# An RWKV attention and Hadamard FFN kernel: another order of work at the start, and three sets of weight forms made one block later

## The chip, the cores and the metric

The kernel runs on one core of a Trainium2 chip. A time is that of the whole program on the device, in microseconds (us), and smaller is better. The core has five engines that run their own instruction streams: TensorE (PE, matrix products into the eight PSUM banks), VectorE (DVE), ScalarE (ACT), GpSimd (POOL) and SyncE (SP), which here issues every DMA. Each stream is worked off in its order, and an instruction that waits holds up all that stand behind it on the same engine.

## The reference, cut to what matters

The input is 4 sequences of 2048 tokens with 512 channels, in 32-bit floats. What is computed:

```python
xn = layernorm(x)                                   # over the 512 channels of a token, no weights
shifted = xn of the token before (zero at a sequence's first)
xr, xk, xv = (mu * xn + (1 - mu) * shifted for mu in (mu_r, mu_k, mu_v))
r, k, v = xr @ Wr.T, xk @ Wk.T, xv @ Wv.T           # 512 x 512 each
wkv = a recurrence over the tokens with running maximum, numerator and denominator
attn = (sigmoid(r) * wkv) @ Wo.T
hidden = silu(xn @ W1.T) * (xn @ W3.T)              # 2048 wide
ffn = fwht(hidden) @ W2.T                           # Walsh-Hadamard transform over the 2048
out = x + attn + ffn
```

## The kernel before, in words

The 8192 tokens are worked off in 8 blocks of TB = 1024 tokens; two blocks make a sequence. Channels lie on the partitions, tokens along the free dimension, so `xnT` holds a block as 4 channel groups of 128 by 1024 tokens.

Each large product is done on 2 x 2 quarters with seven products in place of eight (`seven`, `down`). That needs seven *forms* of each weight, four of them the weight's quarters and three or four made by adding and subtracting quarters (`seven_forms` and `forms_in`, four POOL instructions of 128x256 for one tile). A *part* is one tile of seven forms (896 KB): there are 6 for k, v and r (`part_w` rows 0 to 5) and 16 for the FFN's first layer (rows 6 to 21). Forms are made once and kept in DRAM (`part_w`, `down_w`); later blocks load them from there. A part is loaded into `ring_a`, a pool of three buffers, so the load of a part must wait until the part three before it has been read for the last time. `ring_b` is a pool of two larger buffers, through which pass the square weights of block 0, the down weights and the tiles in which forms are made.

A normal block (1 to 7) goes: six calls of `projected_pair` (k, k, v, v, r, r; 14 matmuls each), sixteen of `up` (14 matmuls each), then `down`, seven products of 20 matmuls. During `down`, pieces of the next block's preparation are called between the products (`next_tokens`: statistics, normalizing, mixing), and at the last product `next_parts` loads the next block's first two parts.

Block 0 differs. Its k, v and r are plain products of 4 matmuls per 128x512 output (`projected`, 8 outputs for each of k, v, r). Beside them W2 is folded with the Hadamard matrix: `fold_load` brings W2 in eight pieces of 512 KB into the upper half of `hid`, `fold_products` multiplies each piece by the 128x128 Hadamard matrix `had_sb` (two matmuls a piece, and two ACT instructions that bring the result back), and `fold_butterflies` does the rest of the transform on VectorE. In the `up` loop of block 0 `down_forms` makes the forms of the down weights in steps 0 to 9, and `keep_parts` the six forms of k, v and r in steps 10 to 15: SP loads the quarters into a `ring_b` buffer, POOL makes the forms, SP stores the tile into `part_w`.

The opening works in two halves of 512 tokens. For each, `statistics` takes mean and variance on VectorE with tokens on the partitions, a power on POOL, writes scale and shift for each token to DRAM (`stat_d`) and reads them back broadcast to all partitions (`spread`); `normalize` applies them with two instructions for each channel group (two groups on VectorE, two on POOL), and `mixed(1)` makes k's mixed input in `tf`: for each group one ACT instruction and one VectorE instruction. The second half is normalized when k's products of the first half have been issued (the branch `n == NB`).

The order on each engine is that of the program text: every engine is wrapped in `InOrder`, which keeps program order. PSUM banks are given out in turn, eight of them. The profile puts every instruction on line 34, the line of that wrapper, so groups are told apart by their tiles: `bank<-tf,w` is k in block 0, `bank<-hid,w` v and r, `bank<-hid,had_sb` the folding, `bank<-xnT,part` and `bank<-tf,part` the `up` products, `bank<-hid,dw` the down products.

Of the kernel before, what the change touches and what calls it, by code (L numbers as in the profile page):

```python
# [8 lines left out]
F32 = mybir.dt.float32  # L9
AF = mybir.ActivationFunctionType  # L10
ALU = mybir.AluOpType
# [3 lines left out]
P = 128  # L15
# [24 lines left out]
def tile_rwkv_attn_hadamard_ffn(  # L40
# [7 lines left out]
    w2: bass.AP,  # L48
    wo: bass.AP,
    had: bass.AP,  # L50
    outT: bass.AP,
    n_batch: int,
):
# [49 lines left out]
    vec = const.tile([P, 5, NB], F32, name="vec")  # L103
    omm = const.tile([P, 3, NB], F32, name="omm")
    weff = const.tile([P, NB], F32, name="weff")
    had_sb = const.tile([P, P], F32, name="had_sb")
    neg_half = const.tile([P, TP], F32, name="neg_half")
    carry = const.tile([P, NB, 3], F32, name="carry")


    def load_tokens(i, t0=0, n=TB):
        dst = x_tok[:, t0 // P : (t0 + n) // P, :]
        sp.dma_start(out=dst, in_=x[ds(i * TB + t0, n), :].rearrange("(p t) c -> p t c", p=P))

    def load_channels(i, t0=0, n=TB):
        dst = xnT[:, :, OFF + t0 : OFF + t0 + n]
        sp.dma_start(out=dst, in_=xT[:, ds(i * TB + t0, n)].rearrange("(b p) t -> p b t", p=P))

    def statistics(i, t0=0, n=TB):

        m, key = n // P, f"{i}_{t0}"
        st = small.tile([P, TP, nc.vector.BN_STATS_DIM], F32, tag="st", name=f"st_{key}")
        mv = small.tile([P, TP, nc.vector.BN_AGGR_DIM], F32, tag="mv", name=f"mv_{key}")
        rs = small.tile([P, 2, TP], F32, tag="rs", name=f"rs_{key}")
        for t in range(m):
            dve.bn_stats(out=st[:, t, :], in_=x_tok[:, t0 // P + t, :])
        for t in range(m):
            dve.bn_aggr(out=mv[:, t, :], in_=st[:, t, :])
        dve.tensor_scalar(rs[:, 0, 0:m], mv[:, 0:m, 1], EPS, None, ALU.add)
        pool.tensor_tensor(rs[:, 0, 0:m], rs[:, 0, 0:m], neg_half[:, 0:m], ALU.pow)  # L130
        dve.scalar_tensor_tensor(rs[:, 1, 0:m], mv[:, 0:m, 0], -1.0, rs[:, 0, 0:m], ALU.mult, ALU.mult)
        far = stat_d[i, :, t0 : t0 + n]
        sp.dma_start(out=far.rearrange("s (p t) -> p s t", p=P), in_=rs[:, :, 0:m])
        sp.dma_start(out=spread[:, :, t0 : t0 + n], in_=far.unsqueeze(0).to_broadcast([P, 2, n]))

    def token_before(i):
        if i % per_batch == 0:
# [1 line left out]
        else:  # L139
            dve.tensor_copy(xnT[:, :, OFF - 1 : OFF], xnT[:, :, OFF + TB - 1 : OFF + TB])  # L140

    def normalize(t0=0, n=TB):
        for b in range(NB):
            eng = dve if b < KH else pool
            for s, op in ((0, ALU.mult), (1, ALU.add)):
                xb = xnT[:, b, OFF + t0 : OFF + t0 + n]
                eng.tensor_tensor(xb, xb, spread[:, s, t0 : t0 + n], op)

    def mixed_block(kind, b, t0=0, n=TB):
        m = mix_of[kind][:, b, t0 : t0 + n]  # L150
# [1 line left out]
        act.activation(m, before, AF.Copy, scale=omm[:, kind, b : b + 1])  # L152
        dve.scalar_tensor_tensor(m, here, vec[:, kind, b : b + 1], m, ALU.mult, ALU.add)

    def mixed(kind, t0=0, n=TB):
        for b in range(NB):
            mixed_block(kind, b, t0, n)


    def load_square(i, kind):  # L160
# [142 lines left out]
    def forms_in(t):  # L303
        seven_forms([t[:, n] for n in range(3, 7)], *(t[:, n] for n in range(4)))

    def load_parts(i, n):
        t = ring_a.tile([P, 7, KH, P], F32, tag="a", name=f"part_{i}_{n}")
        if i:
            sp.dma_start(out=t, in_=part_w[n])
        else:  # L310
            sp.dma_start(out=t[:, 0:4], in_=wpart[n])
            forms_in(t)
        return t

    def keep_parts(n):
        t = ring_b.tile([P, 7, KH, P], F32, tag="b", name=f"keep_{n}")
        sp.dma_start(out=t[:, 0:4], in_=wpart[n])
        forms_in(t)
        sp.dma_start(out=part_w[n], in_=t)

    def projected_pair(i, n, w, tail, hook):

        kind, g = (1, 2, 0)[n // KH], n % KH
        dst = (r_sb, k_sb, v_sb)[kind]
        d11, d12, d21, d22 = (dst[:, mh * KH + g, ts(t, H)] for mh in range(2) for t in range(2))

        def out(d, p):
            if kind == 0:
                act.activation(d, p, AF.Tanh, scale=0.5)
            else:  # L330
                act.copy(d, p)

        def on11(pa):
            out(d11, pa)
            hook()

        def on22(pa, pb, s5):
            dve.tensor_tensor(d22, pb, s5, ALU.add)
            hook()

        def on12(pc, s5):
            dve.tensor_tensor(d12, pc, s5, ALU.add)
            hook()

        pb, pc, pd = seven(f"{i}_r{n}", w, right_of[kind], tail, on11, on22, on12)
        left = [lambda: out(d21, pd)]
        if kind == 0:
            left += [lambda: out(d22, d22), lambda: out(d12, d12)]
        return left

    def up(i, j, w, tail, step):


        if i == 0:
            sp.dma_start(out=part_w[3 * KH + j], in_=w)

        h0, h1 = hid[:, j, 0:H], hid[:, j, H:TB]

        def on11(pa):
            act.activation(h0, pa, AF.Tanh, scale=0.5)  # L360

        def on22(pa, pb, s5):
            dve.scalar_tensor_tensor(h0, h0, 1.0, pa, ALU.add, ALU.mult)
            step()
            dve.tensor_tensor(pb, pb, s5, ALU.add)

        def on12(pc, s5):
            dve.tensor_tensor(pc, pc, s5, ALU.add)
            step()

        pb, pc, pd = seven(f"{i}_{j}", w, right_of["up"], tail, on11, on22, on12)
        return (
            lambda: act.activation(h1, pc, AF.Tanh, scale=0.5),
            lambda: dve.tensor_tensor(h0, h0, pd, ALU.mult),
            lambda: dve.scalar_tensor_tensor(h1, h1, 1.0, pc, ALU.add, ALU.mult),
            lambda: dve.tensor_tensor(h1, h1, pb, ALU.mult),
        )
# [142 lines left out]
        product(6, pb, y21, False, c21)  # L520


    load_tokens(0, 0, H)
    sp.dma_start(out=had_sb, in_=had)
    load_channels(0, 0, H)
    sp.dma_start(out=vec, in_=vecs.rearrange("p (v c) -> p v c", v=5))
    w_next = load_square(0, 1)
    pool.memset(neg_half, -0.5)
    statistics(0, 0, H)
    fold_load(0, 2)  # L530
    load_tokens(0, H, H)
    load_channels(0, H, H)
    fold_load(2, 4)
    fold_products(0, 2)
    dve.tensor_scalar(omm, vec[:, 0:3, :], -1.0, 1.0, ALU.mult, ALU.add)
    act.activation(weff, vec[:, 3, :], AF.Exp)
    token_before(0)
    normalize(0, H)
    mixed(1, 0, H)
    statistics(0, H, H)  # L540
    dve.tensor_scalar(weff, weff, -1.0, None, ALU.mult)

    pending = {}
    for i in range(n_blocks):
# [13 lines left out]
        if i == 0:  # L558
            for kind, after in ((1, 2), (2, 0), (0, None)):
                w = w_next  # L560
                if after is not None:
                    w_next = load_square(i, after)
                    if kind != 1:
                        mixed(after)
                if kind == 2:
                    token_forms()
                    fold_load(4, NP)
                for n in range(2 * NB):
                    if kind == 1:
                        if n == NB:  # L570
                            fold_products(2, 4)
                            normalize(H, H)
                            mixed(1, H, H)
                            mixed(2)
                        projected(kind, w, n % NB, n // NB)
                    else:
                        projected(kind, w, n // 2, n % 2)
                    if kind == 2 and n == 2:
                        fold_products(4, NP)
                        folded = fold_butterflies()  # L580
            parts = [load_parts(i, 3 * KH + n) for n in range(2)]
        else:

            def r_chores():
                for b in range(NB):
                    mixed_block(0, b)
                    yield
                yield from mix_forms(0)

            for kind in (1, 2):  # L590
                next(pending[kind])
            chores, hooks = r_chores(), [0]
            for n in range(3 * KH):
                parts.append(load_parts(i, n + 2))
                if n == KH:
                    token_forms()

                def hook():
                    hooks[0] += 1
                    if n <= KH:  # L600
                        next(chores, None)
                    if hooks[0] in (9, 11, 12, 14, 15, 17, 18):
                        step()

                tail = projected_pair(i, n, parts.pop(0), tail, hook)
# [3 lines left out]
        for j in range(NF):  # L609
            if i == 0 and j < NR:  # L610
                down_forms(j, folded)
            if i == 0 and j >= NF - 3 * KH:
                keep_parts(j - NF + 3 * KH)
            if j + 2 < NF:
                parts.append(load_parts(i, 3 * KH + j + 2))
            if j >= NF - 2:
                w_down.append(load_down(i, order[j - NF + 2]))
            tail = up(i, j, parts.pop(0), tail, step)
# [85 lines left out]
```

## Time and profile before

| | us |
|---|---|
| Median of three runs (3148.56 to 3155.57) | 3153.32 |
| The profiled execution | 3154.58 |
| Its span (first to last instruction) | 3152.4 |
| PE busy in it, 7224 matmul records | 3111.9 (99%) |
| DVE busy | 2200.6 (70%) |
| ACT busy | 871.6 (28%) |
| POOL busy | 338.5 (11%) |
| PE's first matmul starts at | 19.14 |
| First `up` product of block 0 starts at | 125.91 |
| First down product of block 0 starts at | 329.36 |

One 128x512 matmul in 32-bit floats shows as two matmul records; in the steady parts records follow one another every 0.43 us, so a matmul takes 0.86 us of PE. "Idle before" is the time for which an engine had nothing to do before an instruction, with what ended it.

### The profile page before, as it was taken

How to read it: one execution, taken by the hardware profiler on the slowest of the kernel's cores; microseconds unless marked ns; L12 is line 12 of the kernel's file. 1: busy time of each engine (PE TensorE's matmuls, PEld its weight loads, DVE VectorE, ACT ScalarE, POOL GpSimd, SP SyncE). 2: the span in 40 equal slices, each digit the busy share in tenths (PEclk: the TensorE clock that was granted, in tenths of full speed). 3: DMA queues.
4: the chain of work that ended last, by engine and by line, in shares of the span. 5: the costliest groups of instructions: out<-in, count | busy, mean ns of one | idle time of the engine just before them, and what ended most of it. 6: DMA issues, size and time to landing. Idle time of an engine off the chain costs nothing.

```text
span 3152.4 us, 20196 instructions
## 1 busy us (share of the span) xinstructions
PE 3111.9 (99%) x7224; PEld 1375.3 (44%) x7224; DVE 2200.6 (70%) x2300; ACT 871.6 (28%) x1366; POOL 338.5 (11%) x210
## 2 busy tenths in 40 slices
PE   6999999999999999999999999999999999999999
PEld 2443444444444444444444444444444444444444
DVE  5798756886478864787647876579655886658852
ACT  3233113331233302333023320333213332133310
POOL 3355301001000011000110001100011000110000
PEclk9999999999999999999999999999999999999999
DMA  4255632233322332223332224222332223322222
GB/s 174 94 167 199 236 107 70 82 125 110 108 81 77 118 127 102 82 70 114 133 107 79 73 102 157 95 70 82 128 124 101 72 82 145 123 74 81 75 101 77
DMA packets 76691, 340.93 MB, mean 108 GB/s; under 512 B 9776, under 2 KB 18864, under 8 KB 66992
## 3 DMA queue, kind: packets, MB, share of 16 engines
q1 hardware_dynamic: 76592, 339.65, 30.7%
q8 instruction: 57, 0.93, 0.1%
q14 instruction: 42, 0.34, 0.0%
HBM read 293.41 MB, written 46.20 MB: 108 GB/s over the span
## 4 chain that ended last, share of the span: by engine, by line
PE 96%; DMA 2%; POOL 1%; DVE 1%; SPq 0%; issue 0%; ACT 0%; POOLq 0%; DVEq 0%
PE bank L34 96%; POOL keep L34 1%; DMA keep<-wpart 0%; POOL part L34 0%; DMA xnT<-xT 0%; DMA part_w<-keep 0%; DMA dw<-down_w 0%; DVE xnT L34 0%; DMA part<-wpart 0%; DMA stat_d<-rs 0%; DMA k_sb<-x 0%; DVE st L34 0%; DMA v_sb<-stat_d 0%; DVE tf L34 0%; SPq L34 0%
## 5 line engine op out<-in xcount | busy, mean ns | idle before, releaser
L34 PE MATMUL bank<-tf,part 128*128 128x512 f32 x2272 | 1043.0, 592 | 0.0
L34 PE MATMUL bank<-hid,dw 128*128 128x512 f32 x1792 | 790.4, 594 | 4.6 <-DMA dw<-down_w 3.9
L34 PE MATMUL bank<-xnT,part 128*128 128x512 f32 x1536 | 723.9, 594 | 6.7 <-DMA part<-wpart 6.7
L34 PEld LDWEIGHTS bank<-tf,part 128*128 128x128 f32 x2272 | 432.0, 190 | 544.6 <-issue 514.3
L34 ACT COPY bank<-bank 128x512 f32<-128x512 f32 x526 | 299.8, 570 | 1261.5 <-PE bank L34 1255.6
L34 PEld LDWEIGHTS bank<-hid,dw 128*128 128x128 f32 x1792 | 341.4, 191 | 435.7 <-issue 432.0
L34 PEld LDWEIGHTS bank<-xnT,part 128*128 128x128 f32 x1536 | 292.0, 190 | 375.9 <-issue 365.7
L34 DVE SCALAR_TENSOR_TENSOR hid<-hid,bank 128x512 f32<-128x512 f32 x256 | 173.9, 679 | 181.6 <-ACT hid L34 181.5
L34 DVE TENSOR_TENSOR hid<-hid 128x1024 f32<-128x1024 f32 (+1 forms) x173 | 222.3, 1311 | 108.0 <-PE bank L34 107.0
L34 PE MATMUL bank<-hid,part 128*128 128x512 f32 x616 | 271.2, 592 | 0.0
L34 DVE RECIPROCAL e1b<-e1b 128x512 f32<-128x512 f32 x64 | 214.1, 3347 | 1.1
L34 PE MATMUL bank<-r_sb,dw 128*128 128x512 f32 x448 | 210.5, 592 | 0.0
L34 DVE TENSOR_TENSOR bank<-bank,s 128x512 f32<-128x512 f32 x256 | 168.0, 690 | 36.5 <-ACT bank L34 25.3
L34 ACT ACTIVATE hid<-bank 128x512 f32<-128x512 f32 x272 | 163.2, 600 | 98.3 <-PE bank L34 79.7
L34 POOL TENSOR_TENSOR rs<-rs,neg_half 128x8 f32<-128x8 f32 (+1 forms) x9 | 13.6, 1510 | 1577.0 <-DVE rs L34 1577.0
L34 DVE TENSOR_TENSOR hid<-hid,bank 128x512 f32<-128x512 f32 x256 | 173.5, 678 | 11.5 <-PE bank L34 7.1
L34 PEld LDWEIGHTS bank<-hid,part 128*128 128x128 f32 x616 | 117.0, 190 | 147.3 <-issue 145.4
L34 DVE SCALAR_TENSOR_TENSOR hid<-xnT,vec,hid 128x1024 f32<-128x1024 f32 x64 | 93.8, 1500 | 100.4 <-ACT hid L34 100.4
L34 PEld LDWEIGHTS bank<-r_sb,dw 128*128 128x128 f32 x448 | 85.1, 190 | 107.1 <-issue 106.7
L34 POOL TENSOR_TENSOR tf<-xnT 128x1024 f32<-128x1024 f32 x16 | 45.5, 2843 | 667.6 <-PE bank L34 667.6
L34 DVE TENSOR_TENSOR v_sb<-bank,v_sb 128x512 f32<-128x512 f32 x32 | 22.0, 688 | 135.9 <-PE bank L34 135.9
L34 ACT COPY s<-bank 128x512 f32<-128x512 f32 x128 | 75.1, 586 | 146.3 <-PE bank L34 146.3
(93 smaller groups left out, 2225.4 us busy)
## 6 DMA issues: line engine op xcount, KB each, us to landing
part<-part_w SPq DMA_DIRECT2D x154, 896.0 KB, 4.6
dw<-down_w SPq DMA_DIRECT2D x56, 1280.0 KB, 6.3
part_w<-part SPq DMA_DIRECT2D x16, 896.0 KB, 7.1
k_sb<-x SPq DMA_DIRECT2D x7, 2048.0 KB, 8.5
xnT<-xT SPq DMA_DIRECT2D x7, 2048.0 KB, 10.3
v_sb<-xT SPq DMA_DIRECT2D x48, 256.0 KB, 3.8
out<-v_sb SPq DMA_DIRECT2D x48, 256.0 KB, 2.0
part<-wpart SPq DMA_DIRECT2D x16, 512.0 KB, 5.4
```

Of the source, the lines that this page charges most:

```text
L34: return self.tc.keep_in_program_order(issue(*args, **kwargs))
```

## The change

Three things change in the program; the `up` parts of block 0 are handled as before.

1. In the opening, the first block's scale and shift no longer pass through DRAM. `first_spread` builds diagonal matrices from them (an identity `eye_sb` times the per-token value: four on VectorE, four on ACT, for each half) and multiplies them by a matrix of ones on TensorE, which leaves the values broadcast to all partitions in two PSUM banks. `first_normalized` then goes channel group by channel group: two VectorE instructions with the PSUM bank as an operand, and at once the mixing of that group. POOL no longer normalizes in the opening. The statistics of the first half are computed from two loads of 256 tokens.
2. W2's pieces are loaded earlier and folded in another order: pieces 0 and 1 are loaded ahead of the first channels, 2 and 3 just behind them, 4 to 7 after the second half's loads. Pieces 0 to 3 are multiplied before k's first product, 4 and 5 between k's halves, 6 and 7 in v.
3. `keep_parts` is no longer called in the `up` loop with a load and forms of its own. The k, v and r parts are made in block 1 instead: `load_parts` there brings the quarters (512 KB) and makes the forms in the ring buffer, and `projected_pair` stores the tile into `part_w`.

```diff
-    def statistics(i, t0=0, n=TB):
+    def token_statistics(key, tok):
...
+    def load_first_tokens(t, m):
+        src = x[ds(t * P, m * P), :].rearrange("(t p) c -> p t c", p=P)
+        sp.dma_start(out=x_tok[:, t : t + m, :], in_=src)
+
+    def first_statistics(half):
+        return token_statistics(f"f{half}", x_tok[:, half * HT : (half + 1) * HT, :])
+
+    def first_spread(half, rs):
+        diag = v_sb[:, half, :].rearrange("p (s t q) -> p s t q", s=2, q=P)
+        for t in range(HT):
+            dve.tensor_scalar(diag[:, 0, t], eye_sb, rs[:, 0, t : t + 1], None, ALU.mult)
+            act.activation(diag[:, 1, t], eye_sb, AF.Copy, scale=rs[:, 1, t : t + 1])
+        pts = []
+        for s in range(2):
+            pts.append(bank())
+            pe.matmul(pts[s], lhsT=ones, rhs=diag[:, s].rearrange("p t q -> p (t q)"), start=True, stop=True)
+        return pts
+
+    def first_normalized(half, pts):
+        for b in range(NB):
+            xb = xnT[:, b, OFF + half * H : OFF + (half + 1) * H]
+            dve.tensor_tensor(xb, xb, pts[0], ALU.mult)
+            dve.tensor_tensor(xb, xb, pts[1], ALU.add)
+            mixed_block(1, b, half * H, H)
...
     def load_parts(i, n):
         t = ring_a.tile([P, 7, KH, P], F32, tag="a", name=f"part_{i}_{n}")
-        if i:
-            sp.dma_start(out=t, in_=part_w[n])
-        else:
+        if is_first(i, n):
             sp.dma_start(out=t[:, 0:4], in_=wpart[n])
             forms_in(t)
+        else:
+            sp.dma_start(out=t, in_=part_w[n])
         return t
-    def keep_parts(n):
-        t = ring_b.tile([P, 7, KH, P], F32, tag="b", name=f"keep_{n}")
-        sp.dma_start(out=t[:, 0:4], in_=wpart[n])
-        forms_in(t)
-        sp.dma_start(out=part_w[n], in_=t)
+    def is_first(i, n):
+        return i == (1 if n < 3 * KH else 0)
+
+    def keep_parts(i, n, t):
+        if is_first(i, n):
+            sp.dma_start(out=part_w[n], in_=t)

     def projected_pair(i, n, w, tail, hook):
+        keep_parts(i, n, w)
...
-    load_tokens(0, 0, H)
+    pool.memset(neg_half, -0.5)
+    pool.memset(ones, 1.0)
+    load_first_tokens(0, 2)
+    load_first_tokens(2, 2)
     sp.dma_start(out=had_sb, in_=had)
+    sp.dma_start(out=eye_sb, in_=eye)
+    sp.dma_start(out=vec, in_=vecs.rearrange("p (v c) -> p v c", v=5))
+    fold_load(0, 2)
     load_channels(0, 0, H)
-    sp.dma_start(out=vec, in_=vecs.rearrange("p (v c) -> p v c", v=5))
+    fold_load(2, 4)
     w_next = load_square(0, 1)
-    pool.memset(neg_half, -0.5)
-    statistics(0, 0, H)
-    fold_load(0, 2)
-    load_tokens(0, H, H)
+    load_first_tokens(HT, HT)
     load_channels(0, H, H)
-    fold_load(2, 4)
+    fold_load(4, NP)
+    act.activation(weff, vec[:, 3, :], AF.Exp)
     fold_products(0, 2)
+    spread_0 = first_spread(0, first_statistics(0))
     dve.tensor_scalar(omm, vec[:, 0:3, :], -1.0, 1.0, ALU.mult, ALU.add)
-    act.activation(weff, vec[:, 3, :], AF.Exp)
+    dve.tensor_scalar(weff, weff, -1.0, None, ALU.mult)
     token_before(0)
-    normalize(0, H)
-    mixed(1, 0, H)
-    statistics(0, H, H)
-    dve.tensor_scalar(weff, weff, -1.0, None, ALU.mult)
+    fold_products(2, 4)
+    first_normalized(0, spread_0)
+    first_rs = first_statistics(1)
...
-                    fold_load(4, NP)
                 for n in range(2 * NB):
                     if kind == 1:
+                        if n == NB - 1:
+                            spread_1 = first_spread(1, first_rs)
                         if n == NB:
-                            fold_products(2, 4)
-                            normalize(H, H)
-                            mixed(1, H, H)
+                            first_normalized(1, spread_1)
+                            fold_products(4, 6)
                             mixed(2)
                         projected(kind, w, n % NB, n // NB)
...
                     if kind == 2 and n == 2:
-                        fold_products(4, NP)
+                        fold_products(6, NP)
                         folded = fold_butterflies()
...
-            if i == 0 and j >= NF - 3 * KH:
-                keep_parts(j - NF + 3 * KH)
```

More of the change, by code (lines that the diff above doesn't have):

```diff
@@ L50, in tile_rwkv_attn_hadamard_ffn @@
     had: bass.AP,
+    eye: bass.AP,
     outT: bass.AP,
@@ L105, in tile_rwkv_attn_hadamard_ffn, with load_tokens @@
     weff = const.tile([P, NB], F32, name="weff")
-    had_sb = const.tile([P, P], F32, name="had_sb")
+    had_sb, eye_sb, ones = (const.tile([P, P], F32, name=n) for n in ("had_sb", "eye_sb", "ones"))
     neg_half = const.tile([P, TP], F32, name="neg_half")
     carry = const.tile([P, NB, 3], F32, name="carry")
-    def load_tokens(i, t0=0, n=TB):
-        dst = x_tok[:, t0 // P : (t0 + n) // P, :]
-        sp.dma_start(out=dst, in_=x[ds(i * TB + t0, n), :].rearrange("(p t) c -> p t c", p=P))
+    def load_tokens(i):
+        sp.dma_start(out=x_tok, in_=x[ds(i * TB, TB), :].rearrange("(p t) c -> p t c", p=P))
     def load_channels(i, t0=0, n=TB):
@@ L117, in load_channels @@
         sp.dma_start(out=dst, in_=xT[:, ds(i * TB + t0, n)].rearrange("(b p) t -> p b t", p=P))
-    def statistics(i, t0=0, n=TB):
-        m, key = n // P, f"{i}_{t0}"
+    def token_statistics(key, tok):
+        m = tok.shape[1]
         st = small.tile([P, TP, nc.vector.BN_STATS_DIM], F32, tag="st", name=f"st_{key}")
@@ L125, in statistics @@
         for t in range(m):
-            dve.bn_stats(out=st[:, t, :], in_=x_tok[:, t0 // P + t, :])
+            dve.bn_stats(out=st[:, t, :], in_=tok[:, t, :])
         for t in range(m):
@@ L131, in statistics @@
         dve.scalar_tensor_tensor(rs[:, 1, 0:m], mv[:, 0:m, 0], -1.0, rs[:, 0, 0:m], ALU.mult, ALU.mult)
-        far = stat_d[i, :, t0 : t0 + n]
-        sp.dma_start(out=far.rearrange("s (p t) -> p s t", p=P), in_=rs[:, :, 0:m])
-        sp.dma_start(out=spread[:, :, t0 : t0 + n], in_=far.unsqueeze(0).to_broadcast([P, 2, n]))
+        return rs
+    def statistics(i):
+        rs = token_statistics(i, x_tok)
+        sp.dma_start(out=stat_d[i].rearrange("s (p t) -> p s t", p=P), in_=rs)
+        sp.dma_start(out=spread, in_=stat_d[i].unsqueeze(0).to_broadcast([P, 2, TB]))
     def token_before(i):
@@ L140, in token_before, with normalize @@
             dve.tensor_copy(xnT[:, :, OFF - 1 : OFF], xnT[:, :, OFF + TB - 1 : OFF + TB])
-    def normalize(t0=0, n=TB):
+    def normalize():
         for b in range(NB):
@@ L145, in normalize @@
             for s, op in ((0, ALU.mult), (1, ALU.add)):
-                xb = xnT[:, b, OFF + t0 : OFF + t0 + n]
-                eng.tensor_tensor(xb, xb, spread[:, s, t0 : t0 + n], op)
+                xb = xnT[:, b, OFF : OFF + TB]
+                eng.tensor_tensor(xb, xb, spread[:, s, :], op)
+    HT = H // P
+    def load_first_tokens(t, m):
[19 more added lines that the diff above has]
+            mixed_block(1, b, half * H, H)
     def mixed_block(kind, b, t0=0, n=TB):
@@ L153, in mixed_block, with mixed @@
         dve.scalar_tensor_tensor(m, here, vec[:, kind, b : b + 1], m, ALU.mult, ALU.add)
-    def mixed(kind, t0=0, n=TB):
+    def mixed(kind):
         for b in range(NB):
-            mixed_block(kind, b, t0, n)
+            mixed_block(kind, b)
     def load_square(i, kind):
@@ L351, in up @@
     def up(i, j, w, tail, step):
-        if i == 0:
-            sp.dma_start(out=part_w[3 * KH + j], in_=w)
+        keep_parts(i, 3 * KH + j, w)
         h0, h1 = hid[:, j, 0:H], hid[:, j, H:TB]
@@ L691 @@
         "had": had,
+        "eye": np.eye(P, dtype=np.float32),
     }
```

## The prediction

> **What bounds the kernel now.** I read the busy shares first, then TensorE's waits, then the timeline of TensorE and of SP where those waits lie.
>
> ```profile
> PE 3111.9 (99%) x7224; PEld 1375.3 (44%) x7224; DVE 2200.6 (70%) x2300; ACT 871.6 (28%) x1366; POOL 338.5 (11%) x210
> ```
>
> TensorE is the bound nearly everywhere: 7224 records at 0.4288 us are 3097.6 us, and no other engine comes near. Only what TensorE loses can be won. Its waits, in total:
>
> ```profile
> PE bank L34 <- DMA hid<-w: 19.1, 1, 19.1
> PE bank L34 <- DMA part<-wpart: 6.7, 4, 4.6
> PE bank L34 <- DVE tf L34: 6.1, 2, 4.0
> PE bank L34 <- DMA dw<-down_w: 3.9, 1, 3.9
> PE bank L34 <- DVE bank L34: 0.7, 1, 0.7
> ```
>
> The first and third lie in the opening, the others between 268 and 351 us; asked for 372 us to the end, the view lists none. So blocks 1 to 7 have nothing to give. TensorE at the end of block 0's `up` loop (start, length, operation):
>
> ```profile
> 268.39 1.88 PE L34 MATMUL bank<-tf,part 128*128 128x512 f32 x4
> 270.82 1.95 PE L34 MATMUL bank<-xnT,part 128*128 128x512 f32 x4 [0.54 <-DMA part<-wpart]
> ...
> 284.41 1.96 PE L34 MATMUL bank<-xnT,part 128*128 128x512 f32 x4 [1.34 <-DMA part<-wpart]
> ...
> 296.92 1.95 PE L34 MATMUL bank<-xnT,part 128*128 128x512 f32 x4 [0.25 <-DMA part<-wpart]
> ...
> 313.78 3.75 PE L34 MATMUL bank<-xnT,part 128*128 128x512 f32 x4 [4.60 <-DMA part<-wpart]
> ...
> 329.36 7.10 PE L34 MATMUL bank<-hid,dw 128*128 128x512 f32 x16 [0.72 <-DVE bank L34]
> ...
> 350.68 10.03 PE L34 MATMUL bank<-hid,dw 128*128 128x512 f32 x16 [3.91 <-DMA dw<-down_w]
> ...
> 370.85 1.45 PE L34 MATMUL bank<-hid,dw 128*128 128x512 f32 x3
> ```
>
> A step of `up` is 28 records, 12.0 us. From 268.39 to 370.85 there are 4 + 4x28 + 80 = 196 records, 84.0 us of work in 102.5 us: **18.4 us lost**, of which 12 are waits and the rest the half clock after the 4.60 and 3.91 us gaps (3.75 and 10.03 us where 1.88 and 7.03 are normal). The cause stands in SP's queue:
>
> ```profile
> 307.72 0.32 SPq L34 DMA_DIRECT2D part_w<-keep  x1
> 308.14 0.37 SPq L34 DMA_DIRECT2D part<-wpart  x1
> ...
> 339.98 0.32 SPq L34 DMA_DIRECT2D part_w<-keep  x1
> 343.55 0.32 SPq L34 DMA_DIRECT2D dw<-down_w  x1
> ```
>
> The part of step 15 is asked for at 308.14, though its buffer was free when step 12 ended (about 283): SP stood at the store of a `keep` tile, which waited for POOL's forms, which waited for that tile's load. The second down weight (343.55) waits in the same way. The opening:
>
> ```profile
> 17.71 5.71 DVE L34 TENSOR_TENSOR xnT<-xnT,v_sb 128x512 f32<-128x512 f32 x4 [7.43 <-DMA v_sb<-stat_d]
> 19.14 5.12 PE L34 MATMUL bank<-hid,had_sb 128*128 128x512 f32 x8 [19.14 <-DMA hid<-w]
> 26.43 14.00 PE L34 MATMUL bank<-tf,w 128*128 128x512 f32 x32 [2.18 <-DVE tf L34]
> 47.83 16.44 PE L34 MATMUL bank<-tf,w 128*128 128x512 f32 x32 [3.96 <-DVE tf L34]
> ```
>
> k's products end and v's begin at 64.1, with 8 folding matmuls (6.86 us) still to come. What matters is when that point comes and what is left after it.
>
> **What the Trainium skill says.** "TensorE: Matmul & The Clock Gate", Part 1: the array falls to half clock after an idle window of about 3.4 us and needs about as long busy to come back. The trace agrees: after 3.96 us idle five weight loads come 0.86 us apart, then 0.43; after 2.18 us none does. How gaps of 2 us with short work between them count is shown by neither. "ScalarE: Activation LUTs", What ACT_TABLE_LOAD costs: an activation takes 186 ns + 0.833 ns an element, 93 more for a pointer operand, and neighbours overlap by 93; here 512 elements take 0.597 us from PSUM and about 0.70 with a pointer, which fits. "VectorE: DVE Perf Modes", Why PSUM operands drop a tier: a two-tensor 32-bit operation is at the base rate anyway, so a PSUM operand costs nothing; 0.688 us for `v_sb<-bank,v_sb` agrees. "GPSIMD Engine Reference", Specifications: POOL shares its SBUF interface with VectorE; a form takes 0.73 us alone and 1.6 beside a busy VectorE.
>
> **End of block 0.** Removed: 6 loads, 24 POOL forms and 6 stores. Steps 10 to 15 keep one load, four forms and one store each. Step 10's load (part 12), now at 265.23, follows the store of about 251.6, lands some 6 us later, and its forms take 3 to 5 us: ready by 263, needed at 270.3. Later loads go out as each buffer comes free, 24 us ahead. So all DMA waits here go, with both half-clock spells. Not all is won. VectorE still holds a recurrence piece of 3.9 us in step 15, behind which comes the addition for which the down product waits 0.72; counted from step 15's start (copy at 5.9, activation 6.5, three VectorE instructions to 8.5, piece to 12.2, addition 12.9) that gap becomes about 1.0. After the loop VectorE has 18.8 us of recurrence left (331.9 to 350.7). Its r output is needed by the down product's second round about 24 us after the start and is ready at 21.4. The last cover is thinner: today the y22 differences begin at 398.51, 69.2 us after the down products start, with 0.45 us of idle before them; TensorE comes 7.2 us earlier to this point and VectorE only some 1.6 (statistics no longer wait for their load), so the first piece is ready at 68.3 and needed at 68.6. I charge 0.4 (0 to 2). End of block 0: -18.4 + 1.0 + 0.4 = **-17.0** (-18.4 to -14.5).
>
> **Block 1.** Six loads of 512 KB replace six of 896, and 24 forms and 6 stores are added. TensorE's steps start at 455.2, 467.2 and so on. Parts 0 and 1: issue 440.8, landed by 447, forms 3 to 7 us each, so 451 and 456 (form 4, made first, is needed 1.7 us into a step). Part 4: issued 479.2, landed by 488, forms done by 491 to 496. `token_forms` (12 to 13.3 us) is queued behind it on POOL and ends by 509 instead of 489; `up` needs it at 527. Part 5 (issued 491.2) stands behind that: forms begin by 509, done by 516; its step starts at 515.2 and needs form 4 at 516.9. A store of a part goes out at its step's start and takes 7.1 us (10.3 at most), less than the 12 until the next load needs the buffer. VectorE is busy 4.5 to 12 of each 12 us here and can bear the sharing. Cost 0 (0 to 2).
>
> **Opening.** In the trace x lands at 5.85, Hadamard at 6.07, the first channels at 9.74, 3 MB at 12.35: about 2.4 us + 3.3 us for each MB queued. With x and the two small matrices ahead, W2's pieces 0 and 1 land at about 7.8 and 9.2 (7 to 10), the channels near 12 to 13. Four matmuls cold and then warm: 5.12 as now, to 12.95. ACT brings the last back at 13.75; then its four diagonals, 128 elements each: by the skill's price 386 ns, 293 apart, so 15.0 (an estimate). The second spread ends at 15.9; folding 2 and 3 follows to 19.35. ACT's mixing stands behind those four results: first at 20.15. Each group now is a chain of two VectorE instructions (1.41), ACT (0.75), VectorE again: 2.8 us a group with its hand-overs, so k's mixed input is complete 20.9 + 3x2.8 + 0.7 = 30.0. (Today the groups are pipelined on three engines; 26.43 to 28.4.) Nine matmuls of the first three k outputs are left then: 37.7 with the clock warm. The second spread waits until ACT has copied the third output and made the diagonals: 40.65. Fourth output and folding 4 and 5: 47.5. ACT's first mixing stands behind the fourth copy, 44.95; four groups: 54.8. Then 13 matmuls: **66.0** instead of 64.1. But only four folding matmuls are left, so 1.9 - 3.43 = **-1.5**. To this come up to two half-clock spells of 2.6 us, one before 30.0 and one before 54.8, where TensorE works 0.86 us in each 2.8. I take one: +1.1. Ends: -3.5 (warm, W2 early) to +5.5.
>
> **Sum.** Span 3152.4 - 17.0 + 0 + 1.1 = 3136.5. The profiled execution took 3154.58, 2.2 more than its span and 1.3 above the median; carried to the median, 3153.32 - 15.9 = **3137.4**.
>
> **Rivals.** (A) The opening pays: both spells, ACT's order worse than reckoned. +4 to +6, and 1 or 2 at the y22 differences: 3141 to 3147. For it: the serial group chain; against: the loss is bounded by the spells. (B) The opening gains: no spell, W2 at 7: 3130 to 3133. (C) Slower: the new k, v, r chain runs late in block 1. Each part is asked for two steps, 24 us, ahead; load 5.4 to 9, forms 3 to 7 make 8 to 16. From 27 us on, each of six parts would cost 3 us of waiting and 2.8 of half clock: +35, about 3172. Only part 5 with `token_forms` in front comes near its limit. (D) W2 ahead delays tokens and channels: hidden anyway, as VectorE's statistics end near 9.3, well before ACT's 15.0.
>
> **How the numbers follow.** Forecast (3133 to 3141) 70 in 100; A 17; B 7; C and unknown losses 6. 0.2%, some 6 us, is about what this kernel's measurement can tell from no change. Under 3147: 0.94; the rest 0.02 and 0.04. The range is 3130 to 3144: it holds forecast and B and the nearer half of A.
>
> **What would show it.** Right: no wait for `part` or `dw` between 255 and 370; `up` steps of 12.0 us through step 15; v's first product near 66 to 69; no TensorE wait in block 1; the down products of block 0 starting near 316 to 322. Wrong: a TensorE wait on POOL's `part` forms in block 1, a wait for `hid` differences of 3 us or more in block 0's down products, or v starting after 72.

## The result and the profile after

The changed kernel takes 3141.41 us (median of 13 executions, 3137.35 to 3151.68), the kernel before 3153.41: a ratio of 0.9964, 95% interval 0.9953 to 0.9976. It is faster by 12 us where 16 had been forecast, and lies inside the stated range.

The times do not scatter around one value. Sorted, they stand at 3137.4 to 3138.7 (six), 3141.4 to 3141.8 (three), 3148.1 (two) and 3151.6 (two). The profiled execution is one of the last: 3151.47 us, span 3149.7, only 2.7 us below the span before. It therefore shows what the kernel can lose, and a second profile, further down, shows what it loses at the median.

TensorE's share and its waits, in the profile of the changed kernel (time in total, number, longest):

```profile
PE 3120.0 (99%) x7232; PEld 1377.4 (44%) x7232; DVE 2197.9 (70%) x2316; ACT 874.1 (28%) x1374; POOL 330.4 (10%) x203
```

```profile
PE bank L34 <- DVE tf L34: 9.4, 7, 2.1
PE bank L34 <- DMA hid<-w: 8.8, 1, 8.8
PE bank L34 <- DMA part<-wpart: 5.3, 2, 4.3
PE bank L34 <- ACT v_sb L34: 2.0, 2, 1.0
PE bank L34 <- DVE sa L34: 0.2, 1, 0.2
```

Waits add up to 25.7 us where they were 36.5. The wait for W2 fell from 19.1 to 8.8 and those for `dw` and for the addition at the down product are gone; seven waits for `tf` stand where two stood. The waits for parts are still there, but at another place. The timeline of TensorE in the `up` loop (start, length, operation, idle before):

```profile
241.94 1.95 PE L34 MATMUL bank<-xnT,part 128*128 128x512 f32 x4 [1.00 <-DMA part<-wpart]
...
258.53 3.75 PE L34 MATMUL bank<-xnT,part 128*128 128x512 f32 x4 [4.34 <-DMA part<-wpart]
...
333.79 7.03 PE L34 MATMUL bank<-hid,dw 128*128 128x512 f32 x16
```

These are steps 9 and 10, ahead of the place of the old waits (steps 12 to 15). After 273.57 no step is late, the down products start without a wait, and the view lists none for block 1. From the first `up` product (132.62) to the first down product are 201.2 us where 16 steps of 12.02 would be 192.3: 8.9 us lost.

The opening, in TensorE's timeline:

```profile
8.84 6.46 PE L34 MATMUL bank<-hid,had_sb 128*128 128x512 f32 x8 [8.84 <-DMA hid<-w]
...
17.15 1.12 PE L34 MATMUL bank<-v_sb,ones 128*128 128x512 f32 x2 [0.99 <-ACT v_sb L34]
...
23.80 1.21 PE L34 MATMUL bank<-tf,w 128*128 128x512 f32 x2 [2.08 <-DVE tf L34]
26.65 2.07 PE L34 MATMUL bank<-tf,w 128*128 128x512 f32 x2 [1.65 <-DVE tf L34]
...
32.37 10.95 PE L34 MATMUL bank<-tf,w 128*128 128x512 f32 x18 [0.78 <-DVE tf L34]
...
60.39 14.03 PE L34 MATMUL bank<-tf,w 128*128 128x512 f32 x26 [1.73 <-DVE tf L34]
74.26 1.02 PE L34 MATMUL bank<-hid,w 128*128 128x512 f32 x2
```

A matmul (two records) that takes 2.07 us with its drain instead of 1.1 is at half clock; between 28 and 36 us the profile gives a granted clock of 0.50. A stretch of such matmuls is called a half-clock spell below, and this opening has two. The 9 matmuls from 32.37 and the 13 from 60.39 take 10.8 and 13.9 us to the next start where 7.7 and 11.1 are normal. v begins at 74.26, the first `up` product at 132.62 instead of 125.91: the opening loses 6.7 us although W2 comes 10 us earlier.

So the profiled execution adds up: -18.4 (the keep waits, all of them) + 8.9 + 6.7 = -2.8, against -2.7 measured.

### The profile page after: what moved, and what is told of

Same layout as the page of the kernel before. It is cut to its first block, busy times and chain, and to the rows that moved or that the text cites. A ratio compares the mean times of both kernels' runs of the same rounds, so it can differ in the third digit from the quotient of the medians.

```text
span 3149.7 us, 20228 instructions
## 1 busy us (share of the span) xinstructions
PE 3120.0 (99%) x7232; PEld 1377.4 (44%) x7232; DVE 2197.9 (70%) x2316; ACT 874.1 (28%) x1374; POOL 330.4 (10%) x203
## 4 chain that ended last, share of the span: by engine, by line
PE 98%; DMA 1%; DVE 1%; ACT 0%; issue 0%; SPq 0%; ACTq 0%
PE bank L34 98%; DMA part<-wpart 0%; DVE xnT L34 0%; DVE tf L34 0%; ACT tf L34 0%; DMA hid<-w 0%; ACT v_sb L34 0%; SPq L34 0%; DVE sa L34 0%; DVE bank L34 0%; DVE v_sb L34 0%; ACT k_sb L34 0%; ACT hid L34 0%; ACTq L34 0%
## 5 line engine op out<-in xcount | busy, mean ns | idle before, releaser
L34 POOL TENSOR_TENSOR rs<-rs,neg_half 128x8 f32<-128x8 f32 x7 | 11.5, 1649 | 1581.6 <-DVE rs L34 1581.6
```

The lines of the kernel that those rows point to most:

```text
L34: return self.tc.keep_in_program_order(issue(*args, **kwargs))
```

## The experiments

The theories are told in the quoted expectations; a number (theory 1, theory 2) is to be read within its own expectation, since a theory that had lost was replaced for the next runs.

**The changed kernel once more.**

> The changed kernel as it is, to see whether its profile is always that of the first execution. Theory 1 (a phase effect): the wait for parts 9 and 10 (1.0 and 4.3 us, 8.9 us lost with the half clock behind them) and the two half-clock spells of the opening come and go from one execution to the next, so that times lie at separate levels between about 3137 and 3152; an execution near 3138 shows no wait for a part after 130 us. Theory 2 (fixed cost): every execution has these waits, the spread has another origin, and this profile shows them again at whatever time it has.

Median 3145.18 us (3141.34 to 3151.95, 8 executions), ratio 0.9975 [0.9965, 0.9985]. Its profile has a span of 3139.9 us, and these are all of TensorE's waits in it:

```profile
PE bank L34 <- DVE tf L34: 9.2, 7, 2.1
PE bank L34 <- DMA hid<-w: 8.3, 1, 8.3
PE bank L34 <- ACT v_sb L34: 2.0, 2, 1.0
```

No wait for a part. `up` starts at 131.71 (5.8 late) and the down products at 323.97, 192.3 later: -18.4 + 5.8 = -12.6, against a span 12.5 below that of before. Theory 1 holds for the part waits: they come and go. Both half-clock spells are in this profile too; that the second of them comes and goes is seen in `opening_alone`, `store_later` and `nudged` below, whose opening is the same and whose profiles have the first spell alone (`up` at 128.01 to 128.51). So the four levels of times fit two things that come or go: the second spell, some 3 us, and late parts, 8.9 us. Neither gives 3138, the spell 3141.5, the parts 3147 to 3148, both 3151.5. Of the 21 executions of this kernel 8 lie above 3146 us, and their common median is 3141.67, the time of this profile.

**The parts of the change alone.** In `opening_alone` the changed kernel loses the moved forms, and so keeps the opening alone:

```diff
     def load_parts(i, n):
-        if is_first(i, n):
+        if i:
+            sp.dma_start(out=t, in_=part_w[n])
+        else:
             sp.dma_start(out=t[:, 0:4], in_=wpart[n])
             forms_in(t)
-        else:
-            sp.dma_start(out=t, in_=part_w[n])
...
+    def keep_parts(n):
+        t = ring_b.tile([P, 7, KH, P], F32, tag="b", name=f"keep_{n}")
+        sp.dma_start(out=t[:, 0:4], in_=wpart[n])
+        forms_in(t)
+        sp.dma_start(out=part_w[n], in_=t)
...
+            if i == 0 and j >= NF - 3 * KH:
+                keep_parts(j - NF + 3 * KH)
```

`end_alone` is the same edit the other way round, made in the kernel before: these lines are taken out of it and those of the changed kernel put in.

> The kernel before with only the k, v and r forms moved to block 1; the old opening stays. Theory 1 (the part waits of steps 9 and 10 come from up starting 3.6 us earlier against the butterflies, a product of the new opening): no wait longer than 1 us for a part from step 9 on, all of the 18.4 us won, 3135 to 3137, little spread. Theory 2 (taking the keep tiles away itself brings the part waits): waits at steps 9 to 11 as in the changed kernel, 3141 to 3147.

> The changed kernel with the k, v and r forms made in block 0 as before, so only the opening is new. Theory 1 (the opening costs by itself, by half clock and by the shift of up): 6 to 7 us later at the first up product and part waits already at steps 9 and 10, in front of those of the keep tiles: 3156 to 3165. Theory 2 (the opening is worth what was forecast, +1, and the rest is chance): 3152 to 3155, first up product at 126 to 128 us.

`end_alone`: 3136.27 us (3134.28 to 3147.92, 6), ratio 0.9947 [0.9936, 0.9959]. Its span is 3134.0, exactly 18.4 below that of before, with `up` from 125.86 and the down products from 318.12; TensorE waits for nothing after the opening:

```profile
PE bank L34 <- DMA hid<-w: 20.3, 1, 20.3
PE bank L34 <- DVE tf L34: 4.3, 2, 2.2
```

`opening_alone`: 3154.16 us (3151.20 to 3159.99, 13), ratio 1.0004 [0.9996, 1.0012]. The time is that of theory 2, first `up` product at 128.01. The 2.1 us that the opening loses there do not reach the end in full: with the keep tiles still in place, the stretch from the first `up` product to the second down product's start takes 222.95 us where it took 224.77. So the whole gain is the moved forms, and in the medians the new opening takes 5 us of it away (3141.41 against 3136.27). Not all of this is the opening's own time: 8 of 21 executions of the changed kernel have times with late parts in them, and at most 1 of 6 of `end_alone`. With the loop repaired in both, below, the difference is 2.4 us. One of the six times of `end_alone`, 3147.92, doesn't fit theory 1, which wanted the part waits to come from the new opening alone.

**The loop of loads and forms.** SP and POOL around step 4, in the profile of the changed kernel:

```profile
182.75 0.45 SPq L34 DMA_DIRECT2D part<-wpart  x1
...
202.57 0.37 SPq L34 DMA_DIRECT2D down_w<-df  x1
203.04 0.45 SPq L34 DMA_DIRECT2D part<-wpart  x1
```

```profile
189.89 5.73 POOL L34 TENSOR_TENSOR part<-part 128x256 f32<-128x256 f32 x4 [7.64 <-DMA part<-wpart]
195.59 1.70 POOL L34 TENSOR_TENSOR df<-hid 128x256 f32<-128x256 f32 x1
197.37 0.73 POOL L34 TENSOR_TENSOR df<-df,hid 128x256 f32<-128x256 f32 x1
198.18 2.70 POOL L34 TENSOR_TENSOR df<-hid,df 128x256 f32<-128x256 f32 x1
200.84 1.71 POOL L34 TENSOR_TENSOR df<-hid 128x256 f32<-128x256 f32 x1
```

SP may not load the next part before it has issued the store of the down forms (202.57); these wait on POOL behind the part's forms, and those wait for the load before. One turn is load + forms + down forms: here 7.1 + 5.7 + 7.0, 20.3 us with the issues, for a step that lasts 12.0. How late the load issued in step j comes, from the step's start (worked out from the two timelines); it is used 24 us after that start and lands 4.3 to 7.1 us after it is issued:

```
step              3    4     5     6     7     8     9    10
before          0.2  1.6   5.3   9.3   8.5   9.8  15.9  19.2
changed         0.2  2.1  10.3  14.4  19.1  23.5  25.6  17.3
changed, again  0.2  1.8   5.5   9.1   8.8   9.8  15.9  12.0
nudged          0.2  3.4  10.7  13.6  18.5  22.2  26.3  18.5
store_later     0.2  0.2   0.2   0.2   0.2   0.2   0.2   0.2
```

The loop was late in the kernel before too. In the profiled execution it fell another 8.2 us behind between steps 4 and 5, against 3.7 in the other execution: one load took 7.1 us, its forms 5.7 and the down forms 7.0, against 5.5, 4.0 and 5.7. It made none of this good as long as down forms were made, that is to step 9. `store_later` takes SP's wait out of the loop:

```diff
-            sp.dma_start(out=far[:, 3:7], in_=t[:, 0:4])
+            return lambda: sp.dma_start(out=far[:, 3:7], in_=t[:, 0:4])
...
-            sp.dma_start(out=far, in_=t)
+            return lambda: sp.dma_start(out=far, in_=t)
...
-            if i == 0 and j < NR:
-                down_forms(j, folded)
+            store = down_forms(j, folded) if i == 0 and j < NR else None
...
             tail = up(i, j, parts.pop(0), tail, step)
+            if store:
+                store()
```

> The changed kernel with one edit: the store of a down form made in step j is issued by SP behind the load and the store of that step's parts, no longer ahead of the load. Theory 1 (SP's load of a part stands behind POOL's forms, so load, part forms and down forms make one loop of 13 to 20 us for a step of 12): no wait for a part from step 0 to 15, up steps of 12.0 us throughout, 3135 to 3142 with only the opening's spread left, and no execution above 3144. Theory 2 (POOL alone is too slow beside VectorE for a step): the part waits stay, same times as the changed kernel.

> The old opening, k, v and r forms in block 1, and the down forms' stores issued behind the parts. Theory 1 (part waits are the late-running loop of loads and forms, whichever opening stands ahead): 3134 to 3137 without any execution above 3140. Theory 2 (the old opening avoids the waits by itself): the same as end_alone, outliers included.

`store_later`: 3138.78 us (3137.66 to 3142.47, 5), ratio 0.9955 [0.9943, 0.9967]; every load from step 1 to 9 within 0.2 us of its step's start, no wait for a part, no time above 3144. With the old opening: 3136.34 (3136.09 to 3136.99, 5), 0.9948 [0.9934, 0.9961], the outlier of `end_alone` gone. Theory 1 in both.

The next three put the late load in by hand: 1 MB of copies within DRAM ahead of the load of step 4.

```diff
+            if i == 0 and j == 4:
+                for n in range(2):
+                    sp.dma_start(out=part_w[n, :, 0:4], in_=wpart[n])
             if j + 2 < NF:
```

> The changed kernel with 1 MB of extra traffic (two 512 KB copies within DRAM) issued by SP ahead of the part's load in step 4 of block 0, which makes this one load some 2 to 3 us later; the copied bytes are overwritten in block 1. Theory 1 (one late load in the loop of loads and forms is enough: it is then late in each step by more until step 10): part waits in every execution, 3146 to 3153, none below 3145. Theory 2 (the loop forgives a late load, the waits have another start): the two or more levels of the changed kernel, half of the executions at or below 3142.

> The same extra traffic with the old opening and the forms in block 1. Theory 1 (the loop, not the new opening, makes the part waits): every execution 8 to 15 us above end_alone's 3136, that is 3144 to 3151. Theory 2 (the waits need the earlier start of up that the new opening brings): 3135 to 3139.

> The same extra traffic in store_later, where SP's load of a part no longer stands behind POOL's down forms. Theory 1: the late load is made good within two steps, no part waits, as store_later within 1 us: 3137 to 3143. Theory 2 (a late load costs wherever it is): above 3145.

`nudged`: 3147.19 us (3145.84 to 3154.17, 13), 0.9982 [0.9974, 0.9990]: no execution below 3145 any more. `end_alone_nudged`: 3145.11 (3144.39 to 3147.27, 7), 0.9975 [0.9964, 0.9986]. `store_later_nudged`: 3138.99 (3138.46 to 3140.17, 5), 0.9953 [0.9940, 0.9967], as without the nudge. TensorE in `nudged`:

```profile
252.81 3.75 PE L34 MATMUL bank<-xnT,part 128*128 128x512 f32 x4 [3.97 <-DMA part<-wpart]
...
269.12 1.95 PE L34 MATMUL bank<-xnT,part 128*128 128x512 f32 x4 [1.28 <-DMA part<-wpart]
```

The first two are as theory 1 says. With either opening, a load that goes out 1.6 us later and takes 7.1 us (179.97 to POOL's first form at 187.08 in `nudged`) brings the late level into every execution. That only the shifted start of `up` can make the waits has fallen: `end_alone_nudged` starts `up` at 125.74 like the kernel before and has them.

The nudges show what one late load does, not why it comes so often in the changed kernel. Times that may hold it are 8 of 21 there, 1 of 6 in `end_alone` (3147.92), 2 of 13 in `opening_alone` (3159.51 and 3159.99) and, over all measurements, 1 of 62 of the kernel before (3161.28). Whether the new opening makes it likelier stays open.

The third says less than I wanted. Without the wait, SP issues the copies already at 169.21, 7.8 us ahead of the load at 176.98, and this load lands in 4.3 us: the copies never met it. That the loop is cured rests on the rows of the table above and on the times: of the 33 executions of the seven kernels with the later store (this one, the two above and the four below) none lies more than 4.9 us above the fastest of its kernel, where a late loop would add 8.9.

**The opening.** In each half every channel group passes VectorE (normalizing), ACT and VectorE again (mixing) before TensorE can use it. `kept_warm` is `store_later` with spare matmuls in TensorE's gaps in this chain; they compute nothing that is used:

```diff
         for b in range(NB):
+            if kind == 1 and h == 0:
+                for _ in range(2):
+                    pe.matmul(banks[7], lhsT=ones, rhs=v_sb[:, half, 0:H], start=True, stop=True)
             pe.matmul(
```

> store_later with two spare matmuls (ones times a diagonal, into a bank that nobody reads) ahead of each of the four matmuls of k's first output in either half: work that leaves nothing in the output and only fills TensorE's gaps of 2 us. Theory 1 (the sparse matmuls of the group chain let the clock fall to half): both half-clock spells go, first up product at 125.3 to 126, 3133.5 to 3136, one level of times instead of two. Theory 2 (the clock falls for another reason, or the spare matmuls only push): first up product at 128.4 or later, 3137 to 3142.

3138.35 us (3137.56 to 3138.54, 5), 0.9954 [0.9941, 0.9966]. The nine matmuls that took 10.95 us in the changed kernel, in its timeline:

```profile
29.67 1.88 PE L34 MATMUL bank<-v_sb,ones 128*128 128x512 f32 x4
31.56 7.99 PE L34 MATMUL bank<-tf,w 128*128 128x512 f32 x18
39.39 1.02 PE L34 MATMUL bank<-v_sb,ones 128*128 128x512 f32 x2
```

The clock half of theory 1 holds: both spells are gone and the second level of times (3142.4 in `store_later`) with them. Its time does not: the first `up` product is at 128.20. In the second half the spare matmuls stand one behind another without a gap from 49.23 to 58.67; counted from the second spread, the chain takes 17.3 us there and 15.2 in `store_later`, so the filling eats the 2 us that it had brought.

Three more kernels build on `store_later`, each with the edits of the one before. `mix_first` puts ACT's mixing ahead of the four folding results:

```diff
-    fold_products(2, 4)
     first_normalized(0, spread_0)
+    fold_products(2, 4)
...
                         if n == NB - 1:
-                            spread_1 = first_spread(1, first_rs)
+                            first_normalized(1, first_spread(1, first_rs))
                         if n == NB:
-                            first_normalized(1, spread_1)
```

`mix_first_staggered` lets VectorE normalize the next group before it ends the last one's mixing, in `first_normalized`:

```diff
-        for b in range(NB):
-            xb = xnT[:, b, OFF + half * H : OFF + (half + 1) * H]
-            dve.tensor_tensor(xb, xb, pts[0], ALU.mult)
-            dve.tensor_tensor(xb, xb, pts[1], ALU.add)
-            mixed_block(1, b, half * H, H)
+        for b in range(NB + 1):
+            if b < NB:
+                xb = xnT[:, b, OFF + half * H : OFF + (half + 1) * H]
+                dve.tensor_tensor(xb, xb, pts[0], ALU.mult)
+                dve.tensor_tensor(xb, xb, pts[1], ALU.add)
+            if b:
+                mixed_block(1, b - 1, half * H, H)
```

`vector_diagonals` makes all eight diagonals on VectorE, in `first_spread`:

```diff
-            act.activation(diag[:, 1, t], eye_sb, AF.Copy, scale=rs[:, 1, t : t + 1])
+            dve.tensor_scalar(diag[:, 1, t], eye_sb, rs[:, 1, t : t + 1], None, ALU.mult)
```

> store_later with ACT's order changed: normalizing and mixing of the first half ahead of the results of W2's pieces 2 and 3, and of the second half ahead of k's fourth output. Theory 1 (the chain waits 3.2 us in each half only because ACT's mixing stands behind four results or a copy): each half 3 us earlier, first up product at 121.5 to 124.5, 3130 to 3133.5. Theory 2 (the chain is bound by its own length and the wait moves elsewhere): a gain of at most 2 us, 3135 to 3140.

> mix_first, and VectorE normalizes group b+1 before it mixes group b, so that it doesn't stand still for ACT's 0.79 us. Theory 1 (four groups at 2.86 us are a chain of VectorE, ACT, VectorE): a group falls to about 2.1 us, each half another 2 us earlier, 3126 to 3130. Theory 2 (TensorE's order and the second spread set the pace by then): within 1.5 us of mix_first.

> mix_first_staggered with all eight diagonals of a half made by VectorE, none by ACT, so that the second spread doesn't wait for ACT. Theory 1 (the two waits of 0.99 us for ACT's diagonals and the 1 us before k's mixing are on the path): 2 to 4 us less than mix_first_staggered's 3124.6, that is 3120.5 to 3122.5. Theory 2 (TensorE's idle time only moves to the wait for VectorE's groups): 3123.5 to 3125.

| kernel | us | ratio, 95% interval | first `up` product |
|---|---|---|---|
| `store_later` | 3138.78 | 0.9955 [0.9943, 0.9967] | 128.46 |
| `mix_first` | 3132.47 | 0.9934 [0.9922, 0.9947] | 122.03 |
| `mix_first_staggered` | 3124.58 | 0.9910 [0.9897, 0.9924] | 114.95 |
| `vector_diagonals` | 3121.92 | 0.9899 [0.9886, 0.9913] | 111.72 |

The first and the last land where theory 1 has them, the staggered one lower than either theory had it: it shortened the groups and at one stroke removed the spell that the profile of `mix_first` still has in the first half (18 records in 10.65 us; the second half has none there). TensorE's waits in `vector_diagonals`, all of them:

```profile
PE bank L34 <- DMA hid<-w: 7.9, 1, 7.9
PE bank L34 <- DVE tf L34: 1.3, 2, 0.9
```

This kernel beats both that were given: 31.5 us below the one before, 19.5 below the changed one. Against `old_opening_store_later` (3136.34) the new opening is good for 14 us when its links are put in this order; as it was written (`store_later`, 3138.78), it cost 2.4.

## Why the prediction was right, step by step

**End of block 0.** Forecast -17.0, measured -18.4 where the loop stays in time. All DMA waits of the keep tiles went, as said. The two charges fell away. The 0.72 us at the first down product, which I expected to grow to 1.0, was absent in both profiles of the changed kernel and in `end_alone`. I had read it as a wait for step 15's addition on VectorE, because the view names VectorE. But in the profile after, that addition starts at 333.94, behind the down product's 333.79. The kernel before has the load of the first down weight here (issue, and time to landing):

```profile
320.65 0.38 SPq L34 DMA_DIRECT2D dw<-down_w  x1
...
dw<-down_w SPq DMA_DIRECT2D x1, 1280.0 KB, 8.6
```

It lands at about 329.3, and the product starts at 329.36. In `opening_alone`, which keeps the keep tiles, the load goes out at 321.79, takes 8.4 us, and the product starts at 330.29, again named after VectorE. In the changed kernel it goes out at 298.80. So this wait, too, was for a load that stood behind a `keep` store, and it belonged to what the change removes. The thin cover at the y22 differences held: they begin 66.6 us after the down products start (ready at 68.3, as forecast, means a start near 67.1) and TensorE doesn't wait. A slip that changes nothing: the waits in the 18.4 us add up to 11.4, not 12.

**The step that failed** is "all DMA waits here go". It took SP's lateness in steps 5 to 9, which lie ahead of the removed tiles, as a fixed quantity of the trace. I had the numbers (a part landing at 255.93 for a step that begins at 258.2) and did not follow them back: they were the state of a loop whose turn takes longer than a step, so the next execution could be 9 us worse. The sum lacked a term of 0 or 8.9 us, present in 8 of 21 executions. Why a load takes 7.1 us instead of 5.5 in some of them is open.

The sentence on step 10's load, that it "follows the store of about 251.6", was wrong as well, without a cost. I let the load go when SP had issued the store of the part that held the buffer; it must wait until that store has landed, 7.5 us after its issue. In the second profile of the changed kernel the store is issued at 256.28 and the load at 263.86, in `end_alone` the load goes out at 257.96. There its forms are ready at 265.6, still ahead of the step that needs them at 270. In the same way the buffer of step 15's part in the kernel before came free near 286.5 (store issued at 279.26, landed 7.2 us later) and not at 283.

**Block 1.** Forecast 0, measured 0. `token_forms` ends at 498.98 in the profile after and the last part's forms at 503.8, for a step that starts near 514; POOL was earlier than the bound of 516 because the loads took 4.4 us and a part's forms mostly 3.0.

**The opening.** Forecast +1.1 with ends at -3.5 and +5.5. Measured at the first `up` product: +2.1 (`opening_alone`), +5.8 and +6.7. The working was right in kind: ACT's first mixing behind four results (22.24 forecast as 20.15), 2.86 us a group (2.8), the second spread behind ACT's diagonals, the mixing behind the fourth copy. Three terms were too small. W2 arrived at 8.35 in the median execution and 8.84 in the profiled one, not 7.8. The four first matmuls took 6.1 and 6.3 us instead of 5.12, half clock lasting longer there. And of the two spells I charged one, at 2.6; both come in the median execution, at 2.9 and 2.7. The +6.7 lies outside the stated ends. How gaps of 2 us with 0.86 us of work between them count was named as unknown; `kept_warm` shows that the clock stays up when they are filled.

**The rivals.** (A) describes the opening of the median execution, both spells and 3141, without the 1 or 2 us that it added at the y22 differences. Its place on the border of the forecast is why the range held. (B) did not occur: even `opening_alone` shows one spell. (C) did not occur: no wait in block 1. (D) is as said: VectorE's statistics end at 9.6, ACT's diagonals at 17.1.

**The sum by its parts**, for the execution at the median: -18.4 + 5.8 = -12.6, against -17.0 + 1.1 = -15.9. The gain at the end of block 0 was put too low, the loss of the opening too low as well, and the errors partly cancel. That the median lies in the range of 3130 to 3144 is in part luck: among the first 13 executions 4 lie above 3146, among the 8 later ones 4, and the median of those 8 is 3145.18, outside it. The forecast knew nothing of these levels.

## What to carry to other kernels

A load that an in-order queue may issue only behind another engine's result belongs to a loop; add up one turn and compare it with the time of a step, because with a longer turn lateness grows, and a late transfer is not made good until the loop ends. When a chain of small instructions feeds TensorE, ask of every link what it stands behind: here the order on each engine decided between a cost of 2.4 us and a gain of 14. And a gain that was won by removing waits in one place is best measured alone before it is put together with another change.

## What the runs showed of the hardware

TensorE fell to half clock without any idle stretch longer than 2.1 us: with one matmul of 0.86 us in every 2.86 us it fell in the first half of every profile that kept this chain unfilled, within 5 us of the last dense stretch, and in the second half of two out of six (9 matmuls in 10.8 us afterwards instead of 7.7). In `mix_first` gaps of 0.89, 1.74 and 1.73 us still brought the fall (18 records in 10.65 us), in `mix_first_staggered` gaps of 0.45 and 0.86 did not (20 records in 8.87). In `end_alone` k's first products took 15.5 us behind a gap of 2.17 us, in the kernel before 13.8 behind one of 2.18: the same gap can cost or not. The Trainium skill, "TensorE: Matmul & The Clock Gate", Part 1, speaks of an idle window of about 3.4 us; here the clock fell without an idle stretch of that length.

Four ACT instructions of 128 elements with a pointer scale took 1.26 us in the changed kernel (15.84 to 17.10). The estimate from the price in the Trainium skill, "ScalarE: Activation LUTs", What ACT_TABLE_LOAD costs, was 1.27.

Loads of 512 KB that were issued alike in steps 2 to 9 of one execution of the changed kernel took 5.4 to 7.1 us until POOL began their forms. In the profiled execution one of the long ones, with 1.7 us more of POOL's forms behind it, stood at the head of the 8.9 us that this execution lost.
